# Folded biases, q and k by channel, three groups in flight, and 128-row products in a four-layer network

## The chip, the cores and the metric

The kernel runs on one core of a Trainium2 chip. The metric is the time of one execution on the device in microseconds (us); lower is better. A core has five engines that run their own instruction streams in order and meet only at semaphores: TensorE (PE, matrix products into PSUM; PEld is its loading of the stationary operand), VectorE (DVE), ScalarE (ACT), GpSimd (POOL) and SyncE (SP, which here issues DMAs).

## The reference

Four layers run one after the other on x of shape (4, 128, 64, 64): a Mamba block, a hypergraph convolution, and two layers of attention and experts on tokens, t = (4 batches, 4096 tokens, 128 channels). The change touches the first attention and the end of both expert parts:

```python
# layer 2, attention (b: 384 biases)
qkv = (ln(t) @ W.T + b);  q, k, v = qkv[:, :, 0], qkv[:, :, 1], qkv[:, :, 2]   # 128 channels each
q, k = elu(q) + 1, elu(k) + 1
num = q_t . cumsum(k_t v_t^T);  den = q_t . cumsum(k_t)            # causal, over the 4096 tokens
t = t + num / (den + 1e-6)
# layers 2 and 3, experts: 64 experts, each takes 8 tokens of a batch
probs = softmax over tokens (ln(t) @ gate_w.T + gate_b)
pooled[e] = sum of its 8 tokens times their probs
out[e] = weight2[e] . gelu(weight1[e] . pooled[e])                  # with biases
t[token] += out[e] * prob of (token, e), for the 8 tokens of each expert
```

The result of layer 3 is written with channels first, so it is turned on the way out.

## The kernel before, in words

Everything is float32. The activations of layers 2 and 3 stay in SBUF as X[token in block, batch, block, channel]: 4 batches, 32 blocks of 128 tokens. The program text only lists the work: a scheduler orders each engine's instructions from the data they need, the program order and the free buffers of each pool, so a later stage's independent work may stand among an earlier stage's. After that each engine runs its list in order.

**attn2** (first attention) works on groups of G = 4 blocks of one batch. Batches go in pairs; the groups of the two alternate, 16 groups for a pair, 32 in all, and one pair is finished before the next begins. For a group:

- `project`: the norm's mean and rate come from `ln_stats` (L700 to L712, one call for 16 blocks, with a square root on ACT at L711). Each block is normed on DVE (`normed`, L716), turned on PE (L752) and copied by ACT to zT (L753). One product per block gives q, k and v together, tokens down the partitions, 384 columns (L758); DVE adds the bias row (L759). elu(x)+1 is max(x,0) + exp(-relu(-x)): two ACT passes over 1024 columns (L763, L764) and one on DVE (L765).
- `turned`: q and k of every block are turned on PE (L775), 8 turns for a group, and copied by ACT (L778).
- `attend`: scores a = k.q of each block (L784), masked on DVE to AT (L786); the output o is AT times [v, 1] (L792) plus q times the running state S (L794); the state grows by k times [v, 1] in PSUM (L796) and ACT copies it to SBUF for the next block (L801). DVE divides and adds to X (L803 to L807).

The state makes a chain along a batch: product L796, copy L801, then L794 of the next block and the next L796. Each group is projected while the group before it is attended. PSUM has 8 banks: 3 for turns and scores, 3 for products, 2 for the states.

**ffn** ends with the experts' outputs. `obs[p]` holds, for a pair of batches p, 2 x 64 rows (batch r, expert) of 128 channels; `route[p]` has the same rows and the 4096 tokens. Each tile of 4 blocks uses the 64 rows of its batch only: in layer 2 four products of 128 columns (L1144), then an addition to X on DVE (L1145); in layer 3 (`out` given) X is turned by four products with the identity (L1151) and one product of 512 columns adds the experts (L1155), DVE or ACT copies the tile (L1160) and SP sends it out (L1161).

Of the kernel before, what the change touches and what calls it, by code (L numbers as in the profile page):

```python
# [16 lines left out]
P = 128  # L17
B = 4
# [20 lines left out]
class Net:  # L39
# [680 lines left out]
    def attn2(self):  # L720

        nc, tc, a, X = self.nc, self.tc, self.a, self.X
        G = 4
        with ExitStack() as ctx:
            wp = ctx.enter_context(tc.tile_pool(name="a2w", bufs=1))
            sp = ctx.enter_context(tc.tile_pool(name="a2s", bufs=4))
            tp = ctx.enter_context(tc.tile_pool(name="a2t", bufs=3))  # L730
            ps = ctx.enter_context(tc.tile_pool(name="a2ps", bufs=3, space=PSUM))
            sps = ctx.enter_context(tc.tile_pool(name="a2n", bufs=1, space=PSUM))

            wT = wp.tile([P, 3, P], F32, tag="wT", name="wT2")
            w = wp.tile([P, 3, P], F32, tag="w", name="w2")
            nc.sync.dma_start(w, a["L2_attn_W"].rearrange("(k p) c -> p k c", p=P))
            pt = ps.tile([P, 3, P], F32, tag="tr", name="ps_w2")
            for k in range(3):
                nc.tensor.transpose(pt[:, k, :], w[:, k, :], self.ident)
            nc.vector.tensor_copy(wT, pt)  # L740
            bias = wp.tile([P, 3 * P], F32, tag="bias", name="bias2")
            nc.sync.dma_start(bias, a["L2_attn_b_row"].to_broadcast([P, 3 * P]))

            def project(b, g, nm, rs):

                zT = tp.tile([P, G, P], F32, tag="zT", name="zT2")
                pt = ps.tile([P, G, P], F32, tag="tr", name="ps_z2")
                for i in range(G):
                    j = G * g + i
                    z = sp.tile([P, P], F32, tag="z", name="z2")  # L750
                    self.normed(z, b, j, nm, rs, j % 16)
                    nc.tensor.transpose(pt[:, i, :], z, self.ident)  # L752
                nc.scalar.copy(zT, pt)  # L753
                qkv = tp.tile([P, G, 3 * P + 1], F32, tag=f"qkv{b % 2}", name="qkv")
                nc.gpsimd.memset(qkv[:, :, 3 * P :], 1.0)
                for i in range(G):
                    pq = ps.tile([P, 3 * P], F32, tag="qkv", name="ps_qkv")
                    nc.tensor.matmul(pq, zT[:, i, :], wT.rearrange("p k c -> p (k c)"), start=True, stop=True)  # L758
                    nc.vector.tensor_tensor(qkv[:, i, : 3 * P], pq, bias, ALU.add)  # L759

                qk = qkv[:, :, : 2 * P]
                ex = tp.tile([P, G, 2 * P], F32, tag="ex", name="ex")
                nc.scalar.activation(ex, qk, AF.Relu, scale=-1.0)  # L763
                nc.scalar.activation(ex, ex, AF.Exp, scale=-1.0)  # L764
                nc.vector.scalar_tensor_tensor(qk, qk, 0.0, ex, ALU.max, ALU.add)  # L765
                return qkv

            def turned(b, qkv):

                qkT = tp.tile([P, G, 2, P], F32, tag=f"qkT{b % 2}", name="qkT")  # L770
                for h in range(2):
                    pt = ps.tile([P, 2, 2, P], F32, tag="tr", name="ps_qkT")
                    for i in range(2):
                        for k in range(2):
                            nc.tensor.transpose(  # L775
                                pt[:, i, k, :], qkv[:, 2 * h + i, k * P : (k + 1) * P], self.ident
                            )
                    nc.scalar.copy(qkT[:, 2 * h : 2 * h + 2, :, :], pt)  # L778
                return qkT

            def attend(b, g, qkv, qkT, pS, S):
                pa = ps.tile([P, G, P], F32, tag="tr", name="ps_a")
                for i in range(G):
                    nc.tensor.matmul(pa[:, i, :], qkT[:, i, 1, :], qkT[:, i, 0, :], start=True, stop=True)  # L784
                AT = tp.tile([P, G, P], F32, tag="AT", name="AT")
                nc.vector.tensor_tensor(AT, pa, bc(self.causal, G), ALU.mult)  # L786
                for h in range(2):
                    po = ps.tile([P, 2, 2 * P], F32, tag="qkv", name="ps_o2")
                    for i in range(2):
                        j, k = G * g + 2 * h + i, 2 * h + i  # L790
                        o, v1 = po[:, i, : P + 1], qkv[:, k, 2 * P :]
                        nc.tensor.matmul(o, AT[:, k, :], v1, start=True, stop=S is None)  # L792
                        if S is not None:
                            nc.tensor.matmul(o, qkT[:, k, 0, :], S, start=False, stop=True)  # L794
                        if j < NB - 1:
                            nc.tensor.matmul(  # L796
                                pS, qkv[:, k, P : 2 * P], v1, start=j == 0, stop=j == NB - 2,
                                skip_group_check=True,
                            )
                            S = sp.tile([P, P + 1], F32, tag=f"S{b % 2}", name="S")  # L800
                            nc.scalar.copy(S, pS)  # L801
                    rd = sp.tile([P, 2], F32, tag="rd", name="rd")
                    nc.vector.tensor_scalar(rd, po[:, :, P], 1e-6, None, ALU.add)  # L803
                    nc.vector.reciprocal(rd, rd)
                    for i in range(2):
                        x = X[:, b, G * g + 2 * h + i, :]
                        nc.vector.scalar_tensor_tensor(  # L807
                            x, po[:, i, :P], rd[:, i : i + 1], x, ALU.mult, ALU.add
                        )
                return S  # L810

            for p in range(B // 2):
                pS = [sps.tile([P, P + 1], F32, tag=f"S{r}", name=f"ps_S{r}") for r in range(2)]
                S, st, ready = [None, None], {}, None
                for u in [*((g, r) for g in range(NB // G) for r in range(2)), None]:
                    now = ready
                    if u:
                        g, r = u
                        if g % 4 == 0:
                            st[r] = self.ln_stats(sp, 2 * p + r, G * g, 16)  # L820
                        ready = g, r, project(2 * p + r, g, *st[r])
                    if now:
                        g, r, qkv = now
                        b = 2 * p + r
                        S[r] = attend(b, g, qkv, turned(b, qkv), pS[r], S[r])

    def attn3(self):

# [155 lines left out]
    def ffn(self, name, out=None):  # L984
# [8 lines left out]
        with ExitStack() as ctx:  # L993
# [134 lines left out]
            for p in range(B // 2):  # L1128
                pt = ps.tile([P, P], F32, tag="tr", name="ps_ot")
                nc.tensor.transpose(pt, outT[:, 2 * p : 2 * p + 2, :].rearrange("p b e -> p (b e)"), self.ident)  # L1130
                ob = wp.tile([P, P], F32, tag=f"ob{p}", name="ob")
                nc.vector.tensor_tensor(ob, pt, b2, ALU.add)
                nc.vector.tensor_scalar(ob, ob, dens[p], None, ALU.mult)
                obs.append(ob)
            for p in range(B // 2):
                for c in range(NCH):
                    for r in range(2):
                        b, rows = 2 * p + r, slice(r * E, (r + 1) * E)
                        x = X[:, b, 4 * c : 4 * c + 4, :]
                        if out is None:  # L1140
                            po = ps.tile([P, 4, P], F32, tag="ps", name="ps_f")
                            for i in range(4):
                                cs = slice((4 * c + i) * P, (4 * c + i + 1) * P)
                                nc.tensor.matmul(po[:, i, :], route[p][rows, cs], obs[p][rows, :], start=True, stop=True)  # L1144
                            nc.vector.tensor_tensor(x, x, po, ALU.add)  # L1145
                        else:

                            sl = slice(c * CH, (c + 1) * CH)
                            po = ps.tile([P, CH], F32, tag="ps", name="ps_f")
                            for i in range(4):  # L1150
                                nc.tensor.matmul(  # L1151
                                    po[:, i * P : (i + 1) * P], x[:, i, :], self.ident,
                                    start=i == 0, stop=False, skip_group_check=True,
                                )
                            nc.tensor.matmul(  # L1155
                                po, obs[p][rows, :], route[p][rows, sl], start=False, stop=True,
                                skip_group_check=True,
                            )
                            o = tp.tile([P, CH], F32, tag="s", name="of")
                            (nc.vector.tensor_copy if r else nc.scalar.copy)(o, po)  # L1160
# [63 lines left out]
```

## Time and profile before

| what | value |
|---|---|
| time before, median of 3 runs | 4474.22 us (4468.59 to 4481.0) |
| profiled execution: its own time, span | 4388.62 us, 4386.8 us |
| granted TensorE clock, mean over the span | 0.901 |
| busy shares of the span | PE 82%, DVE 70%, POOL 56%, ACT 47% |
| first attention, about 3400 to 3695 us of the span | PE busy 271.5, DVE 265.5, ACT 168.5 us in the window 3400 to 3697 |
| end of layer 2's experts | 3917 to 3948 us |
| end of layer 3's experts | 4317 to 4384 us |

Busy time counts an instruction from its start to its end, and PE's products overlap, so a PE that is busy all the time may still not start a product as often as it could; starts in the timeline tell that. An idle time in the table of groups is put down to the engine whose signal came last. "128\*128" after PE is rows by columns of the array that a product uses.

### The profile page before, as it was taken

Reading aid. Unit: us, or ns where it says so; the run is one execution under the profiler, and the core shown is the slowest. Engines: PE = TensorE matmul, PEld = TensorE weight load, DVE = VectorE, ACT = ScalarE, POOL = GpSimd, SP = SyncE. Lnnn points to the kernel's source line nnn. Section 1 sums busy time; section 2 is a strip of 40 time slices with the busy share of each in tenths; the row PEclk is TensorE's granted clock in tenths of the full one; section 3 lists DMA queues with packets and bytes.
Section 4 is the critical chain, followed back from the end, with each engine's and each line's share of the span. In section 5 each row is a group of like instructions: output and inputs, shape, how many; then the busy total and the mean of one; then the engine's idle time right before and its main releaser. Section 6 shows DMA issues by size and latency. Waiting matters only on the chain. (4 is left out here: it accounts for less than half of the span.)

```text
span 4386.8 us, 49410 instructions
## 1 busy us (share of the span) xinstructions
PE 3581.4 (82%) x17495; PEld 1997.4 (46%) x17495; DVE 3068.5 (70%) x4945; ACT 2045.6 (47%) x3337; POOL 2465.3 (56%) x1258
## 2 busy tenths in 40 slices
PE   6877758888896888889688888899996899578768
PEld 2333333444543344454334445355653676347534
DVE  5988889997667999766799986744201988428721
ACT  4655654555544445554444556311422564308421
POOL 5999888897787989778788877810003000003100
PEclk8988878899997889999788999999997999799879
DMA  3554545555374445437445553621235000070045
GB/s 104 149 150 147 147 111 134 130 143 135 100 217 113 133 133 139 138 105 210 115 125 136 136 135 104 197 91 63 68 98 204 5 1 2 27 282 3 2 148 199
DMA packets 261737, 524.17 MB, mean 119 GB/s; under 512 B 21962, under 2 KB 24306, under 8 KB 261490
## 3 DMA queue, kind: packets, MB, share of 16 engines
q1 hardware_dynamic: 250194, 501.65, 39.8%
q10 hardware_dynamic: 11296, 19.37, 1.3%
q8 instruction: 138, 2.26, 0.2%
q14 instruction: 109, 0.89, 0.1%
HBM read 443.34 MB, written 77.59 MB: 119 GB/s over the span
## 5 line engine op out<-in xcount | busy, mean ns | idle before, releaser
L284 POOL TENSOR_TENSOR db<-dx,bt 128x1024 f32<-128x1024 f32 x512 | 1203.2, 2354 | 335.0 <-DVE hs L302 219.1
L302 DVE TENSOR_TENSOR_SCAN hs<-hs,carry,db 128x512 f32<-128x512 f32 x812 | 1036.8, 1284 | 173.8 <-ACT hs L296 91.4
L296 ACT ACTIVATE hs<-dl,A 128x512 f32<-128x512 f32 x1024 | 706.6, 692 | 747.5 <-DVE ho L312 693.9
L497 PE MATMUL ps_g<-xn 128*128 128x512 f32 x1152 | 606.4, 657 | 101.3 <-DVE inc L500 77.1
L319 POOL TENSOR_TENSOR ho_s<-ho_s,ho 128x1024 f32<-128x1024 f32 x288 | 677.2, 2351 | 13.7 <-DVE ho L312 13.0
L312 DVE TENSOR_TENSOR ho<-hs,bt 128x1024 f32<-128x1024 f32 x464 | 564.4, 1217 | 1.6
L520 PE MATMUL ps_ed<-xs,inc 128*128 128x258 f16 x4096 | 511.0, 285 | 19.5 <-DVE inc L500 8.8
L520 PEld LDWEIGHTS <-inc 128*128 128x128 fp8e4 x4096 | 416.3, 102 | 134.9 <-issue 62.1
L500 DVE SCALAR_TENSOR_TENSOR inc<-ps_g,hcl,hb 128x512 fp8e4<-128x512 f32 x576 | 421.8, 739 | 39.1 <-PE ps_g L497 23.4
L497 PEld LDWEIGHTS ps_g<-xn 128*128 128x128 f32 x1152 | 216.8, 205 | 420.5 <-DVE inc L500 187.2
L340 PE MATMUL ps_y<-ho,cst 128*128 128x512 f32 x512 | 275.3, 681 | 108.6 <-POOL ho L308 91.4
L620 PE MATMUL ps_v<-inc_v,es 128*128 128x512 fp8e4 x1536 | 342.8, 382 | 20.0 <-DMA bt<-bcd 17.3
L620 PEld LDWEIGHTS <-es 128*128 128x128 f16 x2048 | 202.5, 99 | 289.1 <-issue 63.7
L513 ACT CAST inc<-ps_t 128x512 fp8e4<-128x512 f32 x448 | 232.1, 600 | 95.5 <-PE ps_t L509 95.5
L222 PE MATMUL ps_c<-xt,wc 128*128 128x512 f32 x512 | 234.5, 612 | 10.6 <-DVE inc L500 6.8
L340 PEld LDWEIGHTS ps_y<-ho,cst 128*128 128x128 f32 x512 | 105.5, 215 | 269.7 <-POOL ho L308 121.8
L526 ACT COPY ed<-ps_ed 128x129 f32<-128x129 f32 x128 | 34.0, 266 | 379.7 <-PE ps_ed L520 379.7
L527 DVE TENSOR_TENSOR ed<-ps_ed,ed 128x129 f32<-128x129 f32 x128 | 36.8, 288 | 211.0 <-ACT ed L526 207.9
L302 DVE TENSOR_TENSOR_SCAN hs<-hs,db 128x512 f32<-128x512 f32 x116 | 141.3, 1224 | 53.6 <-POOL db L284 42.6
L536 POOL TENSOR_TENSOR ed<-ed,rdeg 128x512 f32<-128x512 f32 x32 | 33.3, 1039 | 251.1 <-DVE rdeg L532 251.1
L872 POOL MEMSET G<- 128x128 f32 x2 | 0.4, 204 | 300.8 <-PE ps_f L1144 300.8
L222 PEld LDWEIGHTS ps_c<-xt,wc 128*128 128x128 f32 x512 | 99.4, 197 | 136.8 <-issue 116.7
(283 smaller groups left out, 5700.9 us busy)
## 6 DMA issues: line engine op xcount, KB each, us to landing
bt<-bcd SPq DMA_DIRECT2D x512, 512.0 KB
inc<-inc SPq DMA_DIRECT2D x192, 256.0 KB
inc_v<-inc SPq DMA_DIRECT2D x96, 512.0 KB
w<-in_L_ffn_weight SPq DMA_DIRECT2D x32, 1024.0 KB
w2f<-in_L_ffn_weight SPq DMA_DIRECT2D x32, 1024.0 KB
strip<-inc SPq DMA_DIRECT2D x84, 256.0 KB
x<-x ACTq DMA_DIRECT2D x32, 256.0 KB
xn<-x SPq DMA_DIRECT2D x32, 256.0 KB
```

The source lines that it names most:

```text
L222: nc.tensor.matmul(s["ps"][h], wc[:, h, j, :], xt[:, j : j + T], start=j == 0, stop=j == 3)
L284: nc.gpsimd.tensor_tensor(db, s["dx"], bc(s["bt", n][:, 0, :], 2), ALU.mult)
L296: act(nc.scalar.activation(hs[:, k, :], s["dl"][:, k, :], AF.Exp, scale=A[:, k, n : n + 1]))
L302: nc.vector.tensor_tensor_scan(to[:, h, :], hs[:, h, :], db[:, h, :], init, ALU.mult, ALU.add)
L312: nc.vector.tensor_tensor(ho, hs, ct, ALU.mult)
L319: nc.gpsimd.tensor_tensor(s["sum", n // G], s["sum", n // G], ho, ALU.add)
L340: nc.tensor.matmul(s["y"][h], self.ident, t[:, h, :], start=False, stop=n == DS - 1 and k == len(terms) - 1,)
L497: nc.tensor.matmul(pq, xn[v // 4][:, v % 4 * P : (v % 4 + 1) * P], xn[c], start=True, stop=True)
L500: nc.vector.scalar_tensor_tensor(inc[:, v, :], pq, hc[:, v : v + 1], hb, ALU.subtract, ALU.is_gt, saturate=False)
L513: later(1, lambda: act(nc.scalar.copy(inc[:, v, :], pt, saturate=False)))
L520: nc.tensor.matmul(pe[:, : 2 * P + 2], inc[:, v, i * P : (i + 1) * P], xs[:, v, :], start=v == 0, stop=v == NB - 1,)
L620: nc.tensor.matmul(pv, es[:, e, k, :], inc[:, e, :], start=e == 0 and k == 0, stop=e == NB - 1 and k == 1,)
```

## The change

In `attn2`:

- The bias and the "+1" trick: the normed z gets 1 added, so its channels sum to 128; W's rows get (b - sum of the row)/128 added. W.z then has the bias in it, and the addition L759 is gone. Half of the z are made by ACT, half by DVE.
- q and k are made by channel: weights stationary, the group's 512 tokens moving, one product each. v is still made by token. q and k need no turning for the scores and for q.S; k alone is turned back by PE (4 turns a group) and copied by ACT for the state. elu+1 now reads PSUM, 512 columns at a time.
- One loop over all 32 groups in place of one for each pair: group u is projected, u-1 scored, u-2 attended. One pool of 6 banks for all but the states; the pool of SBUF tiles has 4 in place of 3 buffers. The ones beside v are written once to five v buffers.

In `ffn`: `obs[p]` becomes 128 rows x 2 x 128, zero where the row's batch and r differ, so that products use all 128 rows: in layer 2 a product of 256 columns gives both batches of one block, in layer 3 one product of 512 columns as before.

```diff
-            def project(b, g, nm, rs): ... (qkv by token, + bias, elu+1, as described)
-            def turned(b, qkv): ... (8 turns, 2 copies)
+            nc.vector.reduce_sum(r3, w, axis=AX.X)
+            nc.vector.tensor_tensor(r3, bw, r3, ALU.subtract)
+            nc.vector.tensor_scalar(r3, r3, 1.0 / C, None, ALU.mult)
             for k in range(3):
+                nc.vector.tensor_scalar(w[:, k, :], w[:, k, :], r3[:, k : k + 1], None, ALU.add)
                 nc.tensor.transpose(pt[:, k, :], w[:, k, :], self.ident)
+            def norms(b, g):
+                nm, rs = self.ln_stats(sp, b, G * g, 16)
+                nb = sp.tile([P, 16], F32, tag="lnnb", name="lnnb")
+                nc.vector.tensor_tensor(nb, nm, rs, ALU.mult)
+                nc.vector.tensor_scalar(nb, nb, 1.0, None, ALU.add)
+            def project(u):
...
+                    if i % 2:
+                        nc.scalar.activation(z[:, i, :], x, AF.Identity, scale=r, bias=m)
+                    else:
+                        nc.vector.tensor_scalar(z[:, i, :], x, r, m, ALU.mult, ALU.add)
+                    nc.tensor.transpose(pt[:, i, :], z[:, i, :], self.ident)
+                nc.scalar.copy(zT, pt)
+                for k in range(2):
+                    pq = ps.tile([P, G, P], F32, tag="ps", name="ps_qk")
+                    nc.tensor.matmul(pq, wT[:, k, :], zT, start=True, stop=True)       # 512 columns
+                    nc.scalar.activation(ex[:, k, :, :], pq, AF.Relu, scale=-1.0)
+                    nc.scalar.activation(ex[:, k, :, :], ex[:, k, :, :], AF.Exp, scale=-1.0)
+                    nc.vector.scalar_tensor_tensor(qk[:, k, :, :], pq, 0.0, ex[:, k, :, :], ALU.max, ALU.add)
+                for i in range(G):
+                    nc.tensor.matmul(pv[:, i, :], zT[:, i, :], wT[:, 2, :], start=True, stop=True)
+                nc.scalar.copy(v[:, :, :P], pv)
+            def score(u):
+                for i in range(G):
+                    nc.tensor.matmul(pa[:, i, :], qk[:, 1, i, :], qk[:, 0, i, :], start=True, stop=True)
+                nc.vector.tensor_tensor(AT, pa, bc(self.causal, G), ALU.mult)
+                for i in range(G):
+                    nc.tensor.transpose(pk[:, i, :], qk[:, 1, i, :], self.ident)
+                nc.scalar.copy(kt, pk)
...
+            for u in range(len(units) + 2):
+                if u < len(units):
+                    project(u)
+                if 0 <= u - 1 < len(units):
+                    score(u - 1)
+                if u >= 2:
...
+                    S[b] = S[b][0], attend(u - 2, *S[b])
# ffn
-                nc.vector.tensor_tensor(ob, pt, b2, ALU.add)
-                nc.vector.tensor_scalar(ob, ob, dens[p], None, ALU.mult)
+                ob = wp.tile([P, 2, P], F32, tag=f"ob{p}", name="ob")
+                nc.gpsimd.memset(ob, 0.0)
+                for r in range(2):
+                    rows = slice(r * E, (r + 1) * E)
+                    nc.vector.tensor_tensor(ob[rows, r, :], pt[rows, :], b2[rows, :], ALU.add)
+                    nc.vector.tensor_scalar(ob[rows, r, :], ob[rows, r, :], dens[p][rows, :], None, ALU.mult)
-                            for i in range(4):
-                                nc.tensor.matmul(po[:, i, :], route[p][rows, cs], obs[p][rows, :], start=True, stop=True)
+                            for i in range(2):
+                                nc.tensor.matmul(po[:, i, :, :], route[p][:, block j + i], obs[p], start=True, stop=True)
-                            nc.tensor.matmul(po, obs[p][rows, :], route[p][rows, sl], start=False, stop=True)
+                            nc.tensor.matmul(po, obs[p][:, r, :], route[p][:, sl], start=False, stop=True)
```

## The prediction

> **What bounds it now.** First the busy time of the stages (columns: stage, its length, then busy us with instruction counts of PE, PEld, DVE, ACT, POOL, then clock, DMA share, GB/s):
>
> ```profile
> 3425.00:3552.00 127.00, 120.21 (x764) 94.62 (x763) 119.19 (x440) 82.60 (x153) 1.57 (x15) 1.00 0.00 1
> 3552.00:3567.00 15.00, 12.21 (x63) 9.36 (x61) 13.30 (x46) 9.93 (x14) 0.10 (x1) 0.89 0.00 0
> 3567.00:3691.00 124.00, 121.59 (x762) 93.94 (x760) 105.13 (x326) 65.60 (x135) 1.05 (x10) 1.00 0.00 1
> ```
>
> In the first attention PE and DVE are both nearly full (95% and 94% in the first pair's part), ACT is at 65%; the 15 us between the pairs hold one group, so about 7 are a drain and refill. Next the groups of that stage, 32 block groups in all:
>
> ```profile
> L758 PE MATMUL ps_qkv<-wT,zT 128*128 128x384 f32 x256 | 100.2, 501 | 1.7 <-ACT zT L753 1.7
> L759 DVE TENSOR_TENSOR qkv<-ps_qkv,bias 128x384 f32<-128x384 f32 x128 | 68.7, 552 | 8.6 <-PE ps_qkv L758 6.9
> ...
> L775 PE MATMUL ps_qkT<-cst,qkv 128*128 128x128 f32 x256 | 39.6, 276 | 4.2 <-DVE qkv L765 4.0
> ...
> L778 ACT COPY qkT<-ps_qkT 128x512 f32<-128x512 f32 x64 | 35.3, 587 | 58.4 <-PE ps_qkT L775 58.3
> ...
> L801 ACT COPY S<-ps_S 128x129 f32<-128x129 f32 x124 | 33.0, 266 | 45.7 <-PE ps_S L796 45.7
> ```
>
> Durations overlap on PE, so its price is read from starts in the timeline:
>
> ```profile
> 3504.33 0.39 PE L796 MATMUL ps_S<-qkv 128*128 128x129 f32 x2
> ...
> 3506.09 1.46 PE L758 MATMUL ps_qkv<-wT,zT 128*128 128x384 f32 x4
> 3507.38 0.38 PE L775 MATMUL ps_qkT<-cst,qkv 128*128 128x128 f32 x2
> ```
>
> Four instructions of 384 columns take 3507.38 - 3506.09 = 1.29, 0.32 each: 0.84 ns a column. A group's columns on PE are 512 (z turns), 3072 (qkv, two instructions a product), 1024 (qk turns), 1024 (scores) and 3 x 1032 (o twice, state) = 8728, or 7.33 us. Starts of the mask L786 lie mostly 8.1 to 9.4 apart in the first pair and 8.36 in the second. So **PE bounds the stage**, with about 1 us of waits a group. Then layer 3's end:
>
> ```profile
> 4321.86 1.12 PE L1155 MATMUL ps_f<-lg,ob 64*128 64x512 f32 x2
> 4322.91 0.97 PEld L1151 LDWEIGHTS ps_f<-cst,X 128*128 128x128 f32 x8 [0.76 <-issue]
> 4322.91 1.16 PE L1151 MATMUL ps_f<-cst,X 128*128 128x128 f32 x8
> 4323.09 0.69 DVE L1160 COPY of<-ps_f 128x512 f32<-128x512 f32 x1 [4.35 <-PE ps_f L1155]
> 4324.00 0.29 PEld L1155 LDWEIGHTS ps_f<-lg,ob 64*128 64x128 f32 x2
> ```
>
> A tile takes 2.14 (4321.86 to 4324.00) for 1024 + 1024 columns = 1.72. The missing 0.42 lies at the two changes between 64\*128 and 128\*128, about 0.2 each, and no engine is named for it ("issue"). And layer 2's end, all 64\*128:
>
> ```profile
> 3918.88 1.75 PE L1144 MATMUL ps_f<-ob,lg 64*128 64x128 f32 x16 [0.23 <-DVE X L1145]
> 3920.07 1.28 DVE L1145 TENSOR_TENSOR X<-X,ps_f 128x512 f32<-128x512 f32 x2 [0.65 <-PE ps_f L1144]
> 3920.82 1.56 PEld L1144 LDWEIGHTS ps_f<-ob,lg 64*128 64x128 f32 x16 [0.38 <-DVE X L1145]
> ```
>
> Two tiles take 1.94: product of one PSUM buffer (1.19 to the addition's start), addition (0.69), return of the buffer.
>
> **What the Trainium skill says.** "TensorEngine Tiling (Array Packing)", Key Properties: changing the tiling mode drains TensorE. The trace agrees: 0.2 us at each change in layer 3's end. "FP8 and Floating Point Precision", TensorE Precision Notes: true FP32 takes four passes; here two instructions of 0.84 ns a column each for a product. "ScalarE: Activation LUTs", What ACT_TABLE_LOAD costs: about 1283 ns a load, and about 93 ns for each pointer operand of an ACTIVATE; the trace has loads of 1283 ns (L711, L764) and 494 ns for L905, ACT's norm of 128x128 in the second attention, with two pointers.
>
> **The change, part by part.** The built change's order of instructions shows the schedule, no times.
>
> *PE, attention.* q and k by channel move 4 x 512 columns, v 4 x 2 x 128: 3072 as before. Only four turns go: -512 columns, -0.43 a group, leaving 6.90.
>
> *DVE.* Gone: four L759 (2.21) and two of four L716 (0.68). L765 at 1.22 becomes two of 512 columns from PSUM, taken at 0.69 like L786. The norms gain two small operations per 16 blocks. About -2.7 a group: from 8 to some 5.3.
>
> *ACT.* Gone: two L778 (1.17). Added: k's copy and v's copy at 0.59 each, two norms at 0.49, 0.2 for four 512-column passes in place of two of 1024. +1.2 on some 5.5 (82.60 over 15 groups), so 6.7 a group: next in line behind PE.
>
> *POOL and SP.* 32 small memsets become five; the bias's 192 KB row becomes 384 single words ahead of the same transfers in SP's order. No DMA works in the stage (share 0.00); like L851's words in the second attention they should land within 3 us, behind the first eleven statistics on DVE (2.2 us in the trace); each us later moves the start by as much.
>
> *The waits that remain on PE.* In the new order a group runs q, k, v, scores, k turns, then o, state and q.S with the next group's z turns between. From a state product (3504.33) to the load that takes the copied state it is 0.77 (3505.10 in the timeline), the product 0.1 later. Between them PE has a state product, an o and two turns, 0.65: a wait of 0.2, twice a group. q, k and AT come from earlier rounds, so 6.90 + 0.45 = 7.35, taken as 7.4. Queued behind the state copy on ACT are zT and later q's relu; ahead of it k's copy, which by this timetable ends 0.5 before the state product does. A pair of table loads with its root holds ACT for 2.9; before, a group with a pair took 1.2 more (9.33 against 8.11). With ACT fuller I take 1.7. The order has 11 pairs where it had 10; ten after the start: 17 us, 0.57 a group. Average 7.97, an estimate; its ends are 7.1 (waits of 0.2 in all, loads hidden) and 8.8 (waits of 1.3). In PSUM I count at most six live tiles of six, so a late release would hold PE too.
>
> *Start, middle, end.* Ahead of the first norm stand a reduction (0.54 by L853's 0.27 for 128), two tiny operations and three additions (0.2 each), and the norm's two; with three groups in flight the first o product, now at 3425.9, comes about 2.5 later, 3428.4. The pairs join: the order shows no drain. From there 29 x 7.97 = 231.1, and about 11.5 for the last three groups, whose states have little work between them: 3671. The experts' first turns L1043 start at 3694.7 now: **-23.7**.
>
> *Layer 3's end.* No mode change: 31 x 0.42 = -13.0. But the first two tiles' 64-row products ran beside each other (four instructions in 1.13): +0.8. **-12.2**. The copies (0.69 and 0.58 in turn, two PSUM buffers) and the output are hidden: a tile's DMA moves for about 0.8 of 2.14 in the trace.
>
> *Layer 2's end.* Same columns; 256 wide, four instructions a tile in place of eight. The bound is the loop of buffer and addition: 0, -1 to +1 (the addition's address has one dimension more). *obs*: eight half-height DVE operations in place of four, 0.2 ahead of the first product of each layer; memsets on an idle POOL: +0.4.
>
> Sum -23.7 - 12.2 + 0.4 = -35.5 against the profiled execution's 4388.6. That execution lies 1.9% under the median of the timed runs; scaled by 4474.2/4388.6 it is -36: **4438**.
>
> **Rivals.** *ACT hides its work and the waits of 1 us were DVE's:* a group near 7.3 with the loads hidden: 3428.4 + 211.7 + 11.5 = 3651.6, -43 for the attention, 4418. For: DVE's 94%. Against: in the list of waits PE's weight loads wait longer for ACT's state copy (8.5 us at L796, 8.3 at L794) than for DVE's bias addition (9.4).
> *ACT eats the turns:* groups at 8.4: -11 in the attention, 4451. For: ACT at 6.7 with an in-order chain through it.
> *Slower:* ACT becomes the bound. Each of four state copies stands behind a 0.6 us pass, as L801 did behind L764 in the trace; 4 x 0.6 on 6.90 with 0.45 and 0.57 gives 10.3 a group: +45 in the attention, +33 in all, 4507. It decides from 9.2 a group, where the attention loses the 12 that layer 3's end gains. Against: the order puts the copies behind work that is done by then.
> *The tail's gaps are not the mode's:* attention alone, -23, 4450.
>
> **How the numbers follow.** The forecast's case 0.58 (-25 to -46), everything hidden 0.16, turns eaten 0.12, tail unchanged 0.06, slower 0.05, the rest within 0.3% (13 us, about what a measurement of this kernel can tell from no change): 0.03. Faster 0.92, same 0.03, slower 0.05. The range, 4412 to 4462, runs from groups at 7.1 to groups at 8.8.
>
> **What would show it.** Right: masks about 7.4 apart without loads and 9 with; DVE near 70% in the stage; no 15 us gap between pairs; the stage ends near 3671; a tile of layer 3's end at 1.72 with no "issue" wait. Wrong: PE waiting on ACT for over 1.5 a group, on free PSUM tiles, or tiles still at 2.1.

## The result, and the profile after

| | before | after |
|---|---|---|
| median of all runs | 4471.41 us (4419.99 to 4481.0, 4 runs) | 4366.27 us (4352.93 to 4375.8, 4 runs) |
| profiled execution, span | 4388.62, 4386.8 us | 4357.93, 4356.1 us |
| mean TensorE clock | 0.901 | 0.900 |

The change made the kernel faster, by less than 2%: the ratio is 0.987, 95% interval 0.9831 to 0.9909. The ratio leaves out runs over 1.5% above the fastest of their kernel, so it is nearer to 1 than the medians' 0.976.

The medians lie 105 us apart, the two profiled executions only 31. What is between these two numbers turned out to be the larger half of the case. Durations of stages, here and below, come from one profiled execution of each kernel. By stages of the profiled executions (us):

| stage | before | after | difference |
|---|---|---|---|
| start of the first attention (last copy to X ends) | 3400.0 | 3396.8 | -3.2 |
| first attention, to the first turn of the experts' part | 294.7 | 264.6 | -30.1 |
| layer 2: routing, to the first product with w1 | 133.3 | 135.2 | +1.9 |
| layer 2: experts' loop, first to last product with w1 | 82.2 | 82.4 | +0.2 |
| layer 2's end, copy of eo to last addition | 33.7 | 35.8 | +2.1 |
| second attention, to the first turn of layer 3's experts' part | 147.3 | 146.9 | -0.4 |
| layer 3: routing | 131.2 | 131.9 | +0.7 |
| layer 3: experts' loop | 83.1 | 90.9 | +7.8 |
| layer 3's end, copy of eo to last copy out | 69.1 | 59.5 | -9.6 |

First the busy time of the attention's stretches (columns as before: length, PE, PEld, DVE, ACT, POOL, clock, DMA share, GB/s), the kernel after:

```profile
3425.00:3552.00 127.00, 118.86 (x823) 97.78 (x822) 97.75 (x388) 111.39 (x235) 0.00 (x0) 1.00 0.00 1
3552.00:3653.00 101.00, 100.61 (x703) 83.90 (x702) 68.16 (x234) 74.73 (x168) 0.00 (x0) 1.00 0.00 1
```

DVE fell from 94% and 85% in the two parts of before to 77% and 67%; ACT rose from 65% and 53% to 88% in the part with the table loads and 74% in the part without. PE is busy for 94% and 99.6%, and the stretch between the pairs is gone. The groups that answer to those shown of before, from the groups of the attention's window (busy, mean ns, then idle of the engine and who ended it):

```profile
L786 PE MATMUL ps_qk<-zT,wT 128*128 128x512 f32 x128 | 65.6, 623 | 2.2 <-ACT zT L780 2.2
L792 DVE SCALAR_TENSOR_TENSOR qk<-ps_qk,ex 128x512 f32<-128x512 f32 x64 | 43.6, 688 | 31.3 <-ACT ex L791 30.6
L831 ACT COPY S<-ps_S 128x129 f32<-128x129 f32 x124 | 32.8, 266 | 31.0 <-PE ps_S L827 30.1
L810 PE MATMUL ps_k<-cst,qk 128*128 128x128 f32 x128 | 19.2, 273 | 0.0
L812 ACT COPY kt<-ps_k 128x512 f32<-128x512 f32 x32 | 18.7, 586 | 5.7 <-PE ps_k L810 5.7
```

The turns are halved (x128 in place of x256), the bias addition is gone, and DVE now waits for ACT's exponentials, which costs nothing as long as PE does not wait for DVE. The masks (L807) lie 7.51 us apart in the second half of the stage (8.36 before), 5.3 to 9.05 in the part with the table loads, and nowhere 15 apart. Then layer 3's end, from the timeline after:

```profile
4302.21 1.02 PE L1191 MATMUL ps_f<-lg,ob 128*128 128x512 f32 x2
4302.64 0.19 PEld L1187 LDWEIGHTS ps_f<-cst,X 128*128 128x128 f32 x1 [0.24 <-issue]
4303.07 1.05 PE L1187 MATMUL ps_f<-cst,X 128*128 128x128 f32 x8
4303.34 0.69 DVE L1195 COPY of<-ps_f 128x512 f32<-128x512 f32 x1 [3.20 <-PE ps_f L1191]
...
4303.96 1.02 PE L1191 MATMUL ps_f<-lg,ob 128*128 128x512 f32 x2
```

A tile takes 1.75 (4302.21 to 4303.96) in place of 2.14. The "issue" left on the weight loads holds up nothing: the first product with the identity starts 0.86 after the routed product (4303.07 - 4302.21), which is that product's 1024 columns at 0.84 ns. Last, layer 2's end at its start: first the output vectors in the timeline before, then the timeline after:

```profile
3916.21 0.49 DVE L1132 TENSOR_TENSOR ob<-ps_ot,b 128x128 f32<-128x128 f32 x2 [0.42 <-PE ps_ot L1130]
```

```profile
3884.99 0.61 DVE L1164 TENSOR_TENSOR ob<-ps_ot,b 64x128 f32<-64x128 f32 x2 [0.48 <-PE ps_ot L1158]
3885.63 0.60 DVE L1165 TENSOR_SCALAR ob<-ob,den 64x128 f32<-64x128 f32 x2
...
3886.38 6.86 PE L1175 MATMUL ps_f<-ob,lg 128*128 128x256 f32 x22 [1.37 <-DVE ob L1165]
```

Two half-height operations take 0.61, where two full-height ones took 0.49 before; the first product comes 0.7 later than before (PE idle 1.37 in place of 0.67), and its first 22 instructions take 6.86 us because the clock record shows 0.5 for one window of 3.41 us.

### The profile page after: what moved, and what is told of

The parts are those of the page before. It is cut to its first block, busy times and chain, and to the rows that moved or that the text cites. A ratio compares the mean times of both kernels' runs of the same rounds, so it can differ in the third digit from the quotient of the medians.

```text
span 4356.1 us, 49147 instructions
## 1 busy us (share of the span) xinstructions
PE 3553.7 (82%) x17367; PEld 1989.9 (46%) x17367; DVE 3002.4 (69%) x4815; ACT 2084.0 (48%) x3467; POOL 2463.4 (57%) x1235
## 5 line engine op out<-in xcount | busy, mean ns | idle before, releaser
L509 PE MATMUL ps_t<-ident,strip 128*128 128x128 fp8e4 x1344 | 114.8, 227 | 53.5 <-DVE ed L527 18.9
```

## The experiments

**Each part alone.** `attn_alone` has the attention after and the layer ends before; `ends_alone` the reverse.

> Only the first attention is the changed one; the layer ends are those of before. Theory (the gain is the attention's and the third layer's end's, and each stands alone): from the last X copy to the experts' first turn 264.6 +-1.5 us as in the changed kernel (294.7 before), steady masks 7.5 apart; layer 3's end 69 as before, layer 2's end 33.6; some -28 in the profile. Rival (part of the attention's gain comes from the other edits' effect on the schedule): 275 or more. The experts' stretch of layer 3, 83.1 before and 91.0 in the changed kernel: if the half-clock stretch is chance, it may be anything from 82 to 92 here; if it follows from the attention's edit, 91.

Measured: attention 265.0, masks 7.51 apart, layer 3's end 69.0. So far as expected. But layer 2's end took 49.4 in place of 33.7, and with loops of 89.5 and 93.0 us the profiled span was 4388.2: the whole gain of the attention was eaten in an execution whose attention was as fast as it should be. Median 4393.88 (4367.22 to 4455.87, 20 runs), ratio 0.990, 0.9865 to 0.9935.

> Only the layer ends are the changed ones; the first attention is that of before. Theory: attention 294.7 +-1.5; layer 3's end 60 (69.0 before) with a tile at 1.75 and no change of row mode; layer 2's end 35.7 (33.6 before), its first 3.4 us at half clock after a longer idle of PE in front of the products; -7 in all without the experts' stretch. Rival (the gaps of layer 3's end are not the mode's): 67 to 69, tile 2.1. The experts' stretch of layer 3: 82 to 92 if chance, 91 if it follows from the ends' edit.

Measured: attention 294.3; layer 3's end 59.5; layer 2's end 35.9, with 3.4 us at half clock. Median 4402.75 (4370.8 to 4418.31, 17 runs) where the kernel before, on the same chip, had 4466.55 (4400.16 to 4494.76, 36 runs); ratio 0.9924, 0.9893 to 0.9955. The parts are independent: each edited stage takes alone what it takes in the whole. A tile of layer 3's end takes 1.75, so the rival (the tail's gaps are not the mode's) falls. The loop of layer 3 took 89.6 here with the attention of before and 93.0 in `attn_alone` with the ends of before, so neither edit is its cause. The two ends are 7 us shorter in the profile (the span itself is 3 longer, by the loop), the median is 64 lower. That is the open question of the case: some timed runs of the kernel before hold something that its profile does not show.

**What layer 2's end did in `attn_alone`.** Windows of the two ends, first the kernel before, then `attn_alone` (the clock is the number ahead of the last two):

```profile
3917.00:3948.40 31.40, 27.95 (x256) 24.89 (x256) 20.59 (x34) 0.00 (x0) 0.55 (x4) 1.00 0.33 123
```

```profile
3894.40:3941.00 46.60, 45.86 (x256) 44.75 (x256) 22.10 (x35) 0.00 (x0) 0.54 (x4) 0.50 0.21 76
```

The same 256 products, 46.6 us in place of 31.4, at a clock of 0.50 from end to end, with PE busy 98% of the time. "TensorE: Matmul & The Clock Gate" in the Trainium skill, Part 1, says that the clock is either full or half and returns to full after a busy window of about 3.4 us. The clock record here has these two values alone, in stretches of 3.41 us and multiples; but thirteen such windows, with PE busy for 98% of them, did not bring it back, so in this trace being busy is not enough. The theory from here on: **products that use 64 of the 128 rows do not bring the clock back once it is at half; products of 128 rows do.**

Two tries to enter the ends at half clock used copies of DVE ahead of the output vectors:

```diff
             obs = []
+            for _ in range(4):
+                nc.vector.tensor_copy(ch[:, : N // 2], ch[:, N // 2 :])
```

> The changed attention with the layer ends of before (64-row products), and four copies of 128x2048 on DVE ahead of the output vectors, so that PE stands idle some 4 to 9 us before the products of both layer ends and enters them at half clock. Theory (products that use 64 of the 128 rows don't bring the clock back, as in the profile of the attention alone, whose layer 2's end spent 46.6 us at half clock and took 49.4 in place of 33.7): clock 0.5 through the whole of layer 2's end, products to last addition 46 to 48 us in place of 31.5; layer 3's end, where half the columns are 64-row, stays at half too: 40 to 56 us longer than its 69. Rival (that stretch was chance and has nothing to do with the rows): clock 1.00 after one or two windows of 3.4 us, ends 2 to 4 us longer than 31.5 and 69 plus the idle.

> The changed kernel with the same four copies ahead of the output vectors: products of 128 rows after an idle stretch of 4 to 9 us. Theory (128-row products bring the clock back): half clock for one to three windows of 3.4 us, layer 2's end (products to last addition) 33 to 36 us in place of 32.9, layer 3's end 60 plus the idle plus 0 to 4. Rival (rows don't matter): the same share of half clock in both kernels of this pair.

The edit failed of its purpose: the copies hang on nothing in the ends, and the scheduler set them up to a hundred us earlier, so PE's idle time stayed at 0.67 and 1.37. As a further look at both kinds of end the runs still served. `cold_64` kept the full clock in layer 2's end (31.5), and lost it in layer 3's 0.4 us after the first routed product:

```profile
4308.00:4425.00 117.00, 116.92 (x291) 66.08 (x290) 9.72 (x15) 8.78 (x15) 0.00 (x0) 0.50 0.17 65
```

From the first routed product to the last copy that is 123.4 us where the kernel before took 66.9. The starts of the products say the same as the clock record: a tile takes 4.01 in place of 2.14. `cold_128`: 32.8 and 55.4.

The try that held made the idle stretch hang on the data:

```diff
             obs = []
+            for _ in range(24):
+                nc.vector.tensor_scalar(outT, outT, 1.0, None, ALU.mult)
```

> Two edits in stages that don't touch. (1) Layer ends of before (64-row products) behind 24 small operations of DVE on the output vectors' input, so that PE stands idle some 5 to 8 us ahead of the products; this idle stretch hangs on the data and can't be scheduled away. Theory (64-row products don't bring the clock back once it is at half): layer 2's products to last addition 46 to 48 us (31.5 at full clock), layer 3's end 110 to 130 (69 at full clock), clock 0.50 throughout. Rival (chance): back at 1.00 after one to three windows of 3.4 us. (2) The changed attention with its four turns of k issued twice: 512 columns more on PE and nothing else. Theory (PE is the bound): masks 7.94 apart in place of 7.51, 264.8 becomes 277 to 280. Rival (waits for DVE or ACT set the group): 265 to 269.

> Two edits in stages that don't touch. (1) Layer ends of the changed kernel (128-row products) behind the same 24 operations. Theory: half clock for one to three windows of 3.4 us and then 1.00; layer 2's products to last addition 33 to 37, layer 3's end 60 plus the idle of 5 to 8 plus 0 to 4. Rival: half clock throughout, as in the kernel with 64-row products. (2) The changed attention with four added DVE passes of 128x512 per group (result unused), so that DVE has about as much to do as in the kernel before (5.3 becomes some 8.0 a group). Theory (PE is the bound at 7.5, and DVE would be at 8): masks 8.0 to 8.5 apart, 280 to 295, so that the turns alone would have gained next to nothing. Rival (DVE's work was hidden before too): 265 to 268.

The ends (layer 2's, then layer 3's), `idle_64` and then `idle_128`:

```profile
3901.10:3947.70 46.60, 45.89 (x256) 44.79 (x256) 22.12 (x34) 0.00 (x0) 0.48 (x4) 0.50 0.03 13
4326.00:4453.00 127.00, 123.01 (x306) 69.15 (x306) 13.56 (x27) 9.38 (x16) 0.00 (x0) 0.50 0.17 64
```

```profile
3917.00:3950.70 33.70, 32.97 (x128) 23.69 (x128) 22.91 (x38) 0.00 (x0) 0.52 (x4) 0.92 0.02 6
4331.00:4391.00 60.00, 56.98 (x306) 39.93 (x306) 14.41 (x29) 9.37 (x16) 0.00 (x0) 0.94 0.36 133
```

PE stands idle for 8.32 us in both kernels ahead of either end. After it the 64-row ends stay at 0.50 to their last instruction (46.6 and 123.8 us), while the 128-row ends are back at full clock 5.2 and 3.9 us after their first routed product (33.8 and 57.1). That is the theory, and the rival (chance) does not survive it. Layer 3's end has half of its columns in 128-row products, and that half does not suffice either. Over all profiled executions, from the first routed product on:

| | full clock throughout | half clock at or within 1 us of the start, then full | half clock to the end |
|---|---|---|---|
| layer 2's end, 64 rows | 31.5, 31.5 (before, `cold_64`) | none | 46.6, 46.6, 46.2 (`attn_alone`, `idle_64`, `l2_64`) |
| layer 3's end, 64 rows | 66.9, 66.9 (before, `attn_alone`) | none | 123.4, 123.8 (`cold_64`, `idle_64`) |
| layer 2's end, 128 rows | none | 30.5 to 34.2 (9 kernels; half for 3.0 to 6.2 us) | none |
| layer 3's end, 128 rows | 53.5 to 55.4 (5 kernels) | 56.9 to 57.1 (5 kernels; half for 3.3 to 3.9 us) | none |

None of the five 64-row ends that were at half clock came back, and all fourteen 128-row ends did. The number of rows was not varied alone, though: in layer 2 the products also became 256 columns wide in place of 128, and half as many; in layer 3 the changes of mode went with them. The rows are what both ends have in common. A rival for each end alone (narrow products in layer 2, changes of mode in layer 3) was not tested.

**Which end moves the timed runs.** `l2_64` is the kernel after with layer 2's end alone put back to the four 64-row products of a tile:

```diff
-                            for i in range(2):
-                                nc.tensor.matmul(
-                                    po[:, i, :, :].rearrange("p r c -> p (r c)"), route[p][:, (j + i) * P : (j + i + 1) * P],
-                                    obs[p].rearrange("p r c -> p (r c)"), start=True, stop=True,
-                                )
+                            for i in range(4):
+                                cs = slice((4 * c + i) * P, (4 * c + i + 1) * P)
+                                nc.tensor.matmul(po[:, i, :], route[p][rows, cs], obs[p][rows, :], start=True, stop=True)
```

> The changed kernel with layer 2's end as before (64-row products) and layer 3's end as changed (128-row). Timed runs of the kernel before fell in two groups, 4400 to 4434 and 4458 to 4495; the changed kernel's lay in 4353 to 4376. Theory A (the upper group is layer 3's end at half clock, some 50 us): all runs of this kernel in 4350 to 4395, at most the 16 us of layer 2's end apart. Theory B (the upper group is layer 2's end): some runs 40 to 60 us above the others. Rival (the groups belong to the attention): one group at 4353 to 4376.

Measured: layer 2's end at half clock again (46.2), layer 3's end 56.9, and runs from 4358.43 to 4385.4, median 4374.86 (4 runs), ratio 0.9874, 0.9811 to 0.9936. No upper group, and a layer 2's end at half clock made a run of 4381.7, not one 40 to 60 us higher: that speaks for theory A. But four runs are few: `attn_alone`, with both 64-row ends, has only 4 of its 20 runs above 4440, and at that share four runs without one come about by chance in 0.8^4 = 0.41 of all cases. What shows that the upper group hangs on the ends is `ends_alone`. The 36 runs of the kernel before next to it fall into 14 of 4400.16 to 4434.48 and 22 of 4457.67 to 4494.76, and all 17 of `ends_alone`, with the attention of before, lie under 4419. Why the upper group is rarer in `attn_alone` than in the kernel before, with the same ends, is not known.

Which end it is, is arithmetic, for no execution of the upper group was profiled. An end of layer 3 at half clock costs 123.6 - 66.9 = 57, layer 2's end 15, together 72 of the 95 us between the fastest run and the slowest. Their mean clocks of 0.901 and 0.874 make about 260 us more at half clock for the slowest, of which these two ends would hold 170. Outside the two ends the fourteen profiled executions differ by no more than 84 us of half clock (864 to 948), so the rest of the kernel could hold about the remaining 90, but not the 260, unless it strays further in timed runs. What the missing 23 us are is not shown.

**The experts' loop.** In the kernel after, one stretch of layer 3's loop at half clock, and the one before it:

```profile
4205.00:4235.00 30.00, 22.71 (x268) 11.19 (x266) 3.93 (x7) 3.57 (x6) 0.00 (x0) 0.94 0.97 355
4235.00:4269.00 34.00, 29.96 (x196) 12.69 (x196) 3.04 (x5) 2.97 (x5) 0.00 (x0) 0.50 0.86 293
```

In the first stretch DMA sets the pace (share 0.97, PE busy for 76%). At half clock PE is busy for 88% (29.96 of 34.00), the DMA share falls to 0.86, and most groups come 7.5 us apart; only one of them waits for a transfer, for 2.0 us, so PE and its waits for the gelu set the pace there. Over the fourteen profiled executions layer 2's loop took 81.8 to 99.3 us with 13.7 to 65.8 us at half clock, and layer 3's 83.1 to 100.0 with 23.9 to 68.3. `warm` was meant to add two products of 128 rows and 512 columns to each group:

```diff
+                    nc.tensor.matmul(pw, self.ident, route[0][:, :CH], start=True, stop=True)
                     h = tp.tile([P, 4, P], F32, tag="s", name="h")
...
+                    nc.tensor.matmul(pw, self.ident, route[0][:, :CH], start=True, stop=True)
                     hT = tp.tile([P, 4, P], F32, tag="s2", name="hT", bufs=3)
```

> The changed kernel with two added products of 128 rows and 512 columns in each of the 16 groups of the experts' loop, one where PE waits for the gelu, one where it waits for the copy of the turned values; their result is not used. Theory (the experts' products use 32 columns or 4 rows and count too little to hold the clock; the half-clock stretches there are what moves that loop between 82 and 98 us): half-clock time in the loops below 10 us (20 and 38 in the changed kernel), layer 3's loop 82 to 85 in place of 90.9; timed runs closer together than 23 us, median 4340 to 4360. Rival (the half clock comes of the waits for DMA, whatever PE does in between): the same half-clock time, loops 2 to 10 us longer by the added products.

Measured: 55.7 and 37.5 us at half clock, loops 96.1 and 91.7, median 4374.87 (4361.54 to 4387.25, 4 runs), ratio 0.9867, 0.9797 to 0.9937. But this says nothing of the theory, for the added products did not run in the loops. Like the copies of `cold_64` they hang on nothing there, and the scheduler set all of them ahead, into the routing. In layer 2 they start from 3724.1 to 3779.4 (in layer 3 from 4147.0 to 4202.2, ahead of a loop that starts at 4224.1). The last of them, and the first product of the loop with w1:

```profile
3778.97 1.02 PE L1139 MATMUL ps_w<-lg,cst 128*128 128x512 f32 x2
...
3801.09 1.50 PE L1129 MATMUL ps_h<-w,pooled 128*32 128x512 f32 x12 [0.38 <-DVE pooled L1112]
```

So the theory is untested, and what decides the clock in the loop stays open.

**What the attention's gain is made of.** `pairs_apart` runs the schedule of the kernel after once for each pair:

```diff
-            units = [(2 * p + r, g) for p in range(B // 2) for g in range(NB // G) for r in range(2)]
+            for p in range(B // 2):
+                units = [(2 * p + r, g) for g in range(NB // G) for r in range(2)]
```

> The changed kernel with the groups of the two pairs of batch rows scheduled apart: the pipeline of three groups drains and fills again in the middle. Theory (the joined pairs are worth a drain and refill of about 7 us of the 15.2 between two masks in the kernel before): the attention takes 7 to 12 us longer, 272 to 277, with one gap of 14 to 19 between two masks. Rival (PE works through the drain anyway, the gap before was the statistics' and table loads'): 265 to 267.

Attention 271.4: 6.4 to 6.8 longer than in the eight kernels with the same groups, which lie between 264.6 and 265.0. The gap between the masks of its two pairs, from the timeline:

```profile
3533.20 0.68 DVE L807 TENSOR_TENSOR AT<-ps_a,cst 128x512 f32<-128x512 f32 x1
...
3554.08 0.69 DVE L807 TENSOR_TENSOR AT<-ps_a,cst 128x512 f32<-128x512 f32 x1 [1.21 <-PE ps_a L805]
```

20.9 us, over what I gave it, while the stage's cost is just under: the drain of three groups still does work. The theory stands at about 7. (Median 4381.19, 4364.46 to 4387.56, 4 runs; ratio 0.9868, 0.9803 to 0.9933.)

`two_deep` attends a group right behind its scores:

```diff
-            for u in range(len(units) + 2):
+            for u in range(len(units) + 1):
...
-                if u >= 2:
-                    b, g = units[u - 2]
+                if u >= 1:
+                    b, g = units[u - 1]
```

> The changed kernel with two groups in flight in the attention: a group's outputs are issued right behind its scores and turns in place of one group later. Theory (the third group takes the waits for the mask and for the copy of the turned k off PE, about 1 us a group): masks 8.3 to 9.3 apart, attention 290 to 320. Rival (the order of issue is rearranged by readiness, or the waits are filled by the next group's work): 264 to 272.

Attention 285.1, masks 8.22 apart. Its list of waits (us, times, longest), 3430 to 3640:

```profile
PEld ps_o L825 <- ACT S L831: 16.0, 57, 1.1
PEld ps_o L823 <- DVE AT L807: 15.3, 22, 1.1
PE ps_o L823 <- DVE AT L807: 12.3, 26, 0.9
```

PE and its loads wait for the mask (L807), and its loads wait twice as long for the state copy (L831) as in the kernel after (8.1); for the mask they hardly wait there (0.6 in the whole stage). The attention is 5 us under the range given, but the theory holds: the third group in flight is worth 0.71 a group, 20 us in all, the largest of the terms measured here.

Turns and DVE were tried in the two kernels with the long idle stretch, whose other edit lies in the attention. In `idle_64` the four turns of k are issued twice; masks:

```profile
3563.92 0.68 DVE L807 TENSOR_TENSOR AT<-ps_a,cst 128x512 f32<-128x512 f32 x1
3571.86 0.68 DVE L807 TENSOR_TENSOR AT<-ps_a,cst 128x512 f32<-128x512 f32 x1
```

7.95 apart at the median, 0.44 more for 512 columns, which is their time on PE in full; the stage 275.0, 10.2 longer (the table-load groups hide a part). PE is the bound. In `idle_128` DVE gets four more passes a group:

```diff
                     nc.vector.scalar_tensor_tensor(qk[:, k, :, :], pq, 0.0, ex[:, k, :, :], ALU.max, ALU.add)
+                    for _ in range(2):
+                        junk = tp.tile([P, G, P], F32, tag="junk", name="junk", bufs=2)
+                        nc.vector.tensor_tensor(junk, qk[:, k, :, :], ex[:, k, :, :], ALU.add)
```

```profile
3425.00:3552.00 127.00, 121.78 (x850) 101.43 (x849) 117.90 (x371) 103.42 (x224) 0.00 (x0) 1.00 0.00 1
3552.00:3653.00 101.00, 95.22 (x662) 78.93 (x661) 93.03 (x308) 79.63 (x173) 0.00 (x0) 1.00 0.00 1
```

DVE is at 93% and 92%, about as full as in the kernel before. The masks come less evenly, 3.3 to 10.5 apart, but their median in the second half stays 7.51, and the stage is 267.4: 2.5 longer. With three groups in flight the load on DVE is worth no more than that; my theory for this run was wrong and its rival right. Two things it does not show: nothing waits for the added passes, while PE's loads of before waited 9.4 us for the bias addition that the change removed, and DVE's load was not varied with two groups in flight. The three terms (20, 10, 6.8) add up to more than 30: they were taken from the kernel after one at a time, and a wait can be filled by either a turn or another group's work.

**The output vectors, and a better version.** `obs_short` multiplies bias and denominator ahead, so that two full-height operations make a pair's vectors in place of four half-height ones:

```diff
-                    nc.vector.tensor_tensor(ob[rows, r, :], pt[rows, :], b2[rows, :], ALU.add)
-                    nc.vector.tensor_scalar(ob[rows, r, :], ob[rows, r, :], dens[p][rows, :], None, ALU.mult)
+                    nc.vector.scalar_tensor_tensor(
+                        ob[:, r, :], pt, dm[p][:, r : r + 1], ob[:, r, :], ALU.mult, ALU.add
+                    )
```

> The changed kernel, but the experts' output vectors take two operations of 128 rows for a pair of batch rows in place of four of 64 (bias and denominator are multiplied ahead). Theory (the longer idle of PE ahead of the layer ends' products costs them a window at half clock): idle before the first product back to 0.7 or less, clock 1.00 there, layer 2's end 33.0 to 33.8 in place of 35.7, layer 3's end 57 to 58 in place of 60. Rival (the half clock there is chance or comes of something else): clock 0.5 again, and only the idle's 0.7 gained at each end: 35.0 and 59.4.

PE's idle time ahead of layer 2's products fell to 0.49, yet the end took 35.9: the clock was at half from 3884.3, before the idle stretch, for three windows. Layer 3's end took 57.2 (55.4 from the first routed product, at full clock). `cold_128`, with the longer idle stretch of the kernel after, had the full clock in layer 3's end too and the same 55.4. So the length of an idle stretch of about 1 us did not decide whether a window was lost, and my theory that it does is not shown. Median 4369.49 (4364.82 to 4379.99, 4 runs), ratio 0.9855, 0.9781 to 0.9929.

`best` adds to this two more PSUM buffers for the ends:

```diff
-                            po = ps.tile([P, 2, 2, P], F32, tag="ps", name="ps_f")
+                            po = (aps if r else ps).tile([P, 2, 2, P], F32, tag="pf" if r else "ps", name="ps_f")
```

> The changed kernel with the short output vectors and with four PSUM buffers in place of two for the products of the layer ends. Theory (layer 2's end is set by the return of its two buffers, 0.97 a tile against 0.86 of columns on PE): 32 tiles 3 us shorter, 30 to 31 us from the first product to the last addition where no window is at half clock, 32 to 33 with one; layer 3's end 57 to 58. Over all 3 to 6 us less than the changed kernel, less than its timed runs differ among themselves. Rival (two buffers were enough): 33 and 57 to 60.

Additions to X in layer 2's end:

```profile
3926.12 0.69 DVE L1189 TENSOR_TENSOR X<-X,ps_f 128x512 f32<-128x512 f32 x1 [0.18 <-PE ps_f L1184]
3926.98 0.69 DVE L1189 TENSOR_TENSOR X<-X,ps_f 128x512 f32<-128x512 f32 x1 [0.17 <-PE ps_f L1184]
```

0.86 apart, the columns' own time; the stage 30.5 with one window at half clock, layer 3's end 55.3. Both ends together are 6.8 shorter than in the kernel after. In time it can't be told from it: median 4368.41 (4358.65 to 4381.65, 4 runs), ratio 0.9823, 0.9767 to 0.9879, and its profiled loops (99.3 and 98.2) were among the longest.

## Why the prediction was right, and where it was not

The direction and its causes were right: the attention gains by fewer columns and fewer waits on a full PE, layer 3's end by the mode. The size was in part luck. By the ratio the kernel after takes 0.987 x 4474 = 4416, near the range's lower end; by the medians it takes 4366, 72 below the forecast of 4438 and below the whole range. In the profile the stages that the sum was about came to -37.6 against -35.5, but only because two misses cancel: the attention gained 6.4 more than forecast, the two ends 4.3 less. The steps:

- **Carrying the profile to the median** is the step that missed most. I scaled -35.5 by 4474.2/4388.6 to -36, as if the 1.9% between profile and median were spread evenly. The profiled execution of before had both layer ends at full clock; many timed ones, by the arithmetic above, did not, at 57 and 15 us an end. The change did away with that case, which no term of the sum held. Profile against profile the difference was -30.7; the stages that the change does not touch took 7.0 more of it than before.
- **The group**: 7.4 without loads, measured 7.51. The loads were mis-sized: 29 groups took 224.75 us (3424.55 to 3649.30), 7.75 each; less 7.51 that is 0.24 a group, 0.7 to 0.8 for each of nine or ten pairs of loads, where I took 1.7. This is the -30.1 in place of -23.7. Why they cost less is open. It is not the third group: in `two_deep` the masks from the second to the 31st take 3.9 us more than at their steady 8.22, in the kernel after 6.5 more than at 7.51.
- **Start and end of the stage**: first o product 27.75 after the last copy to X, 1.8 later than before (2.5 forecast); drain 12.1 (11.5). The stage itself began 3.2 earlier, in layers that the change does not touch.
- **ACT as the next in line** and the k copy ahead of need: right but for the table loads. PE's loads waited for that copy six times, 5.6 us.
- **DVE near 70%**: 77% and 67%. By `idle_128` DVE's load is worth 2.5 us at most once three groups are in flight, which speaks against the rival that put the waits down to DVE; the wait for the bias addition itself was not tried alone.
- **Layer 3's end**: the tile came to 1.75 (1.72). From the first routed product 66.9 became 56.9, and 55.4 where no window was at half clock; so -10.0 to -11.5 for -12.2, plus 0.4 for the output vectors.
- **Layer 2's end** (0) and **obs** (+0.2 each): +2.1. I priced eight half-height operations by an added 0.2; the first product came 0.7 later, and one window at half clock, which I had not thought of, cost 1.4.
- **The experts' loop** of layer 3, not in the sum at all, took 7.8 more in the profile, with 37.5 in place of 23.9 us at half clock.

## What to carry to other kernels

Ahead of the sum, ask whether the profiled execution is a typical one: if it lies 1.9% under the median, look for a stage that has two durations, and for what keeps it in the longer one. For PE-bound stages with products on half of the rows, filling the other half with zeros costs no columns, and here it took away a state worth up to 57 us. Another group in flight was worth more than the turns that were removed, and with it in place a nearly full DVE cost next to nothing. Before reading an added instruction's effect, look in the timeline for where it ran: two of the edits here were scheduled away from the place that they were meant for.

## What the runs showed of the hardware that was not expected

- At half clock, PE busy for 98% of 46.6 us with 64\*128 products, and 123 us with 64\*128 and 128\*128 in turn, did not return to full clock; ends of 128\*128 products alone did, 3.0 to 6.2 us after the first. At full clock 64\*128 products kept it (31.5 and 66.9 us).
- The price of staying at half clock: 46.6/31.5 = 1.48 in layer 2's end, where PE was busy for 89% at full clock, and 123.6/66.9 = 1.85 in layer 3's, where it was busy for all of 20 us in its middle.
- DVE at 92% of the time next to a nearly full PE (94 to 96%) cost 2.5 us in 265.
- DVE operations on 64 partitions took no less than those on 128: 0.61 us for two of 64x128 against 0.49 for two of 128x128.
